# Layer 0 of a graph network: states sent to DRAM node by node, a ring filled from there, and one tile of states for two early blocks

## The chip, the cores and the metric

The kernel runs on one core of one Trainium2 chip. The metric is the device time of one execution in microseconds; 3351.88 us is the median of three runs of the kernel before (3350.82 to 3364.95). The profile is of one more execution of the same kernel.

## The reference

Four layers over 64 graphs of 256 nodes with 256 features; each layer is followed by a residual sum and a layer norm. Layers 1 to 3 are a graph convolution and two attention layers over whole graphs. The change lies in layer 0, a recurrence over the nodes:

```python
def step(h, i):
    x = jnp.take(h_e, i, axis=1)
    row = jnp.take(norm_adjT, i, axis=1)
    x_par = jnp.einsum('bj,bjd->bd', row, h)
    iou = x @ W_ioux.T + b_ioux + x_par @ W_iouh.T + b_iouh
    r, z = jnp.split(iou, 2, axis=1)
    r, z = (jax.nn.sigmoid(r), jax.nn.sigmoid(z))
    hc = jnp.tanh(x @ W_coux.T + b_coux + x_par * r @ W_couh.T + b_couh)
    h_new = z * x_par + (1.0 - z) * hc
    h = jax.lax.dynamic_update_slice(h, h_new[:, None, :], (0, i, 0))
    return (h, None)
```

Node i needs the sum over all nodes j of adj[j, i] times the state of j, where nodes after i still hold their input x. So the steps can't be taken side by side: each needs the new states of all nodes before it.

## The kernel before, in words

`_recurrence` runs 256 steps, one a node, for all 64 graphs at once. A step's tile is 128 partitions by 128 columns: the 64 graphs twice, once for each half o of the 256 features. A step is a chain over TensorE, ScalarE and VectorE: transpose xp, product for the gate r, sigmoid, transpose, product for the candidate, tanh, and the next xp.

Nodes go in blocks of U = 8 (p is the place of a node in its block) and in tables of T = 32. The sum over earlier states that a node needs is put together from four sources:

- **x side** (`x_side`): nodes that still hold their input. For nodes 128 to 255 it is worked off in gaps between the steps of the first ninety or so nodes.
- **near pushes** (`push`, `push_far`): the last nine or more states, added on VectorE and GpSimd as soon as they exist.
- **late side** (`late`, line 491): for each block, a window of up to 64 states before it, by TensorE matmuls that read the ring Hw. It is done in the places p = 0 to 3 of the block before. Its result goes to DRAM (Lb, line 501) and back in another layout (line 507), and is added at p = 6 and 7 (line 876).
- **early side** (`early_*`, lines 365 to 450): all older states, for a whole table k of 32 nodes at a time. States of a range lo to hi are loaded from DRAM (Hd) into Hs for 8 graphs at once (a "piece" t of 8), the adjacency into A for 16 graphs, multiplied in the places p = 4 to 7, stored to Es and read back later by block. A piece's step number in the list says from when on it may be loaded. Tables 4 and 6 both use states 0 to 80, tables 5 and 7 both 0 to 112; each table loads its own Hs.

The ring Hw holds the last 64 states: 64 rows for graphs 0 to 31 and 64 rows for graphs 32 to 63, one state a partition in each half. A new state hs has the graphs on the partitions, so writing it to the ring turns 64 partitions of 512 bytes into two rows; it takes two DMAs, one for each half of the features (`into_ring`, line 652). Since the late side reads the ring at p = 0 to 3, states are queued in `ring_in` and written two a step at p = 4 to 7. Every 32 steps `flush` (line 634) copies 32 states from the ring to Hd, from where the early side and layers 1 to 3 read them. The last eight states go from hs to Hd.

All these DMAs, but for some at the start, are issued by one queue, SP, in the order of the program. Loads that can wait stand in a list (`load_later`) and are taken two a step at p = 0 to 3 (`next_load`, line 870); stores stand in `transfers` and are issued at the end of a step. The order within a step is written out by hand; nothing moves it. Pools give the buffers: hs has 7, Hs and the layers' weights share 4 of tag "wide".

`_layers` then takes the graphs one by one, several in flight in a fixed rotation; each loads its states from Hd into y (line 1045).

Of the kernel before, what the change touches and what calls it, by code (L numbers as in the profile page):

```python
# [9 lines left out]
F32 = mybir.dt.float32  # L10
# [60 lines left out]
def _recurrence(tc, ident, Hd, x, adj, W_ioux, b_ioux, W_iouh, b_iouh, W_coux, b_coux, W_couh, b_couh, wide, then):  # L71
# [32 lines left out]
    with ExitStack() as ctx:  # L104
# [9 lines left out]
        window = [const.tile([P, T], F32, name=f"window{w}") for w in range(2)]  # L114
        dinv = const.tile([P, N], F32, name="dinv")

        Hw = const.tile([P, HB, D], F32, name="Hw")

        def ring(lo, hi):

# [201 lines left out]
        def x_side():  # L322
# [39 lines left out]

        early = [
            (n, k, lo, hi, t)
            for n, k, lo, hi in (
                (25, 2, 0, 16), (57, 3, 0, 48), (89, 4, 0, 80), (121, 5, 0, 112), (89, 6, 0, 80),
                (153, 6, 80, 144), (121, 7, 0, 112), (185, 7, 112, 176),
            )  # L370
            for t in range(B // GB)
        ]
        early_in = []
        early_pb = []
        early_ub = []
        Es = {}

        def early_load(e, got=[]):

            _, k, lo, hi, t = early.pop(e)  # L380
            rows = hi - lo
            if t == 0:
                Es[k, lo] = dram.tile([2, NG, 4, T, P], F32, name=f"Es_{k}_{lo}", bufs=1)
            Hs = wide.tile([P, GB, D], F32, tag="wide", name=f"Hs_{k}_{lo}_{t}")
            last = [load_later(
                Hs[0:rows], Hd[lo:hi, t * GB:(t + 1) * GB, :], 1
            )]
            if t % 2 == 0:
                A = stream.tile([P, 2 * GB, T], F32, tag="A", name=f"A_{k}_{lo}_{t}")
                last.append(load_later(  # L390
                    A[0:rows],
                    adj[t * GB:(t + 2) * GB, lo:hi, k * T:(k + 1) * T].rearrange("b j i -> j b i"), 1
                ))
                got[:] = [A]
            early_in.append((last, k, lo, hi, t, Hs, *got))

        def early_ahead(n):
            ready = [e for e, piece in enumerate(early) if piece[0] <= n]
            if len(early_in) < 4 and ready:

                half = [e for e in ready if early[e][4] % 2 and early[e - 1:e] != [
                    early[e][0:4] + (early[e][4] - 1,)
                ]]
                early_load((half + ready)[0])

        def early_fill(n):

            if early_pb:
                pb, e = early_pb.pop(), 1
            else:  # L410
                if not early_in or not landed(early_in[0][0], n):
                    return False
                _, k, lo, _, t = early_in[0][0:5]
                pb, e = base_bank([P, 2, D], f"early_{k}_{lo}_{t}"), 0
                early_pb.append(pb)
            _, k, lo, hi, t, Hs, A = early_in[0]
            for q in range(4):
                nc.tensor.matmul(
                    pb[q * T:(q + 1) * T, e, :], A[0:hi - lo, t % 2 * GB + e * 4 + q, :],
                    Hs[0:hi - lo, e * 4 + q, :], start=True, stop=True,  # L420
                )
# [69 lines left out]
        def late(first):  # L491

            k, i = divmod(first, T)
            An = tables[k]["An"]
            lb = stream.tile([P, NG, D], F32, tag="lb", name=f"lb_{first}", bufs=1)
            Lb = dram.tile([2, NG, 4, U, P], F32, tag="Lb", name=f"Lb_{first}")
            sides[first] = blk.tile([P, U, P], F32, tag="late", name=f"late_sb_{first}", bufs=1)

            def send():
                for c in range(2):  # L500
                    nc.sync.dma_start(
                        Lb[c].rearrange("n q u f -> (q u) n f"),
                        lb[i // U::T // U, :, c * P:(c + 1) * P],
                    )

            def receive():
                nc.sync.dma_start(sides[first], Lb.rearrange("c n q u f -> (c n q) u f"))

            def then(n):
                at_step(n, send)  # L510
                at_step(n + 1, receive)

            n = yield
            for u in range(0, NG // 2, 2):
                pb = [base_bank([P, 2, D], f"late_{first}_{u}_{g}") for g in range(2)]
                for e in range(2):
                    for q in range(4):
                        for g in range(2):
                            rows = slice(g * W, (g + 1) * W)
                            b = (u + e) * 4 + q  # L520
                            nc.tensor.matmul(  # L521
                                pb[g][q * T:(q + 1) * T, e, :],
                                An[rows, b].rearrange("p u s -> p (u s)"),
                                Hw[rows, b, :], start=True, stop=True,
                            )
# [105 lines left out]
                    acc[:, 0, :], keep[:, j % 2, :], s, acc[:, 0, :], ALU.mult, ALU.add  # L631
                )

        def flush(lo, hi):

            for lo, hi, at in ring(max(lo, 0), hi):
                for g in range(2):
                    nc.sync.dma_start(
                        Hd[lo:hi, g * HB:(g + 1) * HB, :],
                        Hw[g * W + at:g * W + at + hi - lo],  # L640
                    )

        def state(n):

            h = keep[:, n % 2, :]
            nc.vector.tensor_add(h, zcc, keep[:, 2, :])
            hs = new("hs", n, 7)
            nc.vector.tensor_add(hs, zcc, keep[:, 2, :])
            ring_in.append((n, hs))
            return hs  # L650

        def into_ring():
            n, hs = ring_in.pop(0)
            for o in range(2):
                to = Hw[n % W::W] if n < N - U else Hd[n]
                nc.sync.dma_start(to[..., o * P:(o + 1) * P], hs[o * B:(o + 1) * B])

        def push_far(j, hs, first, count):

# [11 lines left out]
        sides = {}  # L671
        xqT = {}
        pushes = []
        ring_in = []

        tables[0]["S"], double = load_S(0)
        double()
# [79 lines left out]
        for now in range(N):  # L757
# [9 lines left out]
            if n:  # L767

                assert all(j == n - 2 for _, j in pushes)
                hs = state(n - 1)  # L770
                end = min((n - 1) // U * U + 2 * U, N)
                to = list(range(n + 1, end))
                near = to[:len(to) - min(FAR[p], len(to) - 1)] if to else []
                far = to[len(near):]
                pushes += [(m, n - 1) for m in near]
                pushes.sort()
                if p == 0:

                    behind = [(n - 1, hs, m, 4) for m in range(end, min(end + U, N), 4)]

                if p > 3 or n >= N - U:
                    for _ in range(min(2, len(ring_in))):
                        into_ring()
            if p == 0 and U < n + U < N:
                late_side = late(n + U)
                next(late_side)
# [97 lines left out]
                sums_in(n // U + 3)  # L884
            if p == 2 and n // U + 2 < N // U:
                xq[n // U + 2] = load_x(n // U + 2)
            if i == 24:
                flush(n - 8 - T, n - 8)
            if n == N - U + 3:
                assert all(j >= N - U for j, _ in ring_in)  # L890
                flush(N - T // 2, N - U)
            if n == N - 5 * U:
                assert not early and not early_in and not loads
                then(lambda to, of: load_later(to, of, 3))
# [10 lines left out]
                if i == 28:  # L905
                    tables[k + 1]["Sd"] = chain_S(k + 1)
        state(N - 1)
        while ring_in:
            into_ring()


def _layers(tc, ident, Hd, Yd, x, adj, weights, out):
# [16 lines left out]
    with ExitStack() as ctx:  # L929
# [92 lines left out]
        class Graph:  # L1022
# [7 lines left out]
            def load(self):  # L1030
# [11 lines left out]
                            adj[b, :, at:at + 32].rearrange("(i r) c -> r i c", r=32),  # L1042
                        )
                self.y = io.tile([P, 2, D], F32, tag="y", name=f"y_{b}", bufs=7)
                nc.sync.dma_start(self.y, Hd[:, b, :].rearrange("(c p) d -> p c d", p=P))


            def residual_0(self):
# [374 lines left out]
def kernel(ctx: ExitStack, tc: tile.TileContext, ins, out):  # L1423
# [4 lines left out]
    dram = ctx.enter_context(tc.tile_pool(name="dram", bufs=1, space=bass.MemoryType.DRAM))  # L1428
    ident = main.tile([P, P], F32, name="ident")
    make_identity(nc, ident)  # L1430
    Hd = dram.tile([N, B, D], F32, name="Hd")
    l2, l3 = (
        {w + n: ins[f"{l}_gnn_{w}{n}"] for w in "Wb" for n in "vkqo"} for l in ("L2", "L3")
    )
# [55 lines left out]
```

## Time and profile before

| | |
|---|---|
| median of 3 runs | 3351.88 us |
| profiled execution, its own time | 3353.51 us |
| its span | 3351.7 us |
| TensorE busy | 3131.6 us, 93% |
| VectorE busy | 2554.5 us, 76% |
| ScalarE busy | 1838.6 us, 55% |
| GpSimd busy | 1845.0 us, 55% |
| DMA moved | 364.62 MB, 528608 packets |
| queue q1 (SP), share of 16 engines | 39.6% |
| HBM read, written | 240.78 MB, 99.61 MB |

The span is the time from the first to the last instruction of the core. The profile's slices are a fortieth of it, 83.8 us each. In the row of TensorE's busy tenths the first sixteen or seventeen slices are layer 0 and its setup (7 to 9 tenths), the rest layers 1 to 3 (9 tenths). The DMA row is 4 to 8 tenths in layer 0 and 1 to 2 in the layers after it. Busy time says little where a chain of small instructions waits for one another, as in layer 0; there, the lengths of single steps and the waits in them are the thing to read.

### The profile page before, as it was taken

What the parts mean: (1) busy time and instruction counts of PE and PEld (TensorE: products, weight loads), DVE (VectorE), ACT (ScalarE), POOL (GpSimd) and SP (SyncE); (2) the same over time, 40 slices, a digit from 0 to 9 for tenths busy, and PEclk for the clock granted to TensorE, in tenths of its full rate; (3) what the DMA queues carried; (4) which work ended last, traced back from release to release, by engine and by line L of the source; (5) the groups of instructions that cost most, each with busy time, mean ns of one, the idle gap of its engine ahead of it and who ended that gap; (6) DMA issues with size and microseconds to landing.
All of it is one profiled execution on the core that took longest, in us unless ns stands there. A gap on an engine that the chain in (4) does not pass through costs nothing.

```text
span 3351.7 us, 78940 instructions
## 1 busy us (share of the span) xinstructions
PE 3131.6 (93%) x28584; PEld 2311.5 (69%) x28584; DVE 2554.5 (76%) x7381; ACT 1838.6 (55%) x4754; POOL 1845.0 (55%) x2165
## 2 busy tenths in 40 slices
PE   5799998998879998969999999999999999999997
PEld 4566665555545555547888888888888888888885
DVE  3487777776667878856888888888888888888885
ACT  0155554544445544535666666666666666666664
POOL 2377777766667878833444444444444444444443
PEclk7899999999999999989999999999999999999999
DMA  9856685788877675241221211122222222222210
GB/s 292 247 161 156 168 194 152 179 198 207 204 181 178 163 174 152 65 105 47 56 57 54 57 56 54 54 55 58 57 58 58 58 57 58 57 58 58 58 33 20
DMA packets 528608, 364.62 MB, mean 109 GB/s; under 512 B 246620, under 2 KB 494568, under 8 KB 522984
## 3 DMA queue, kind: packets, MB, share of 16 engines
q1 hardware_dynamic: 510520, 342.63, 39.6%
q10 hardware_dynamic: 17696, 16.91, 1.5%
q8 instruction: 229, 3.75, 0.5%
q14 instruction: 163, 1.34, 0.1%
HBM read 240.78 MB, written 99.61 MB: 102 GB/s over the span
## 4 chain that ended last, share of the span: by engine, by line
PE 77%; DMA 8%; DVE 7%; issue 2%; SPq 2%; ACT 2%; POOL 1%; DVEq 0%; ACTq 0%; POOLq 0%
PE mm L997 14%; PE rc L605 6%; PE rc L597 4%; PE s L1195 4%; PE mm_2f L997 3%; PE mm_3v L997 3%; PE mm_3f L997 3%; PE mm_2v L997 3%; PE late L521 3%; PE mm_t L997 3%; PE mm_2s L997 3%; PE mm_g L997 3%; PE mm_2w L997 3%; PE o L1230 3%; DVE ACC L630 3%; PE o L1221 3%
## 5 line engine op out<-in xcount | busy, mean ns | idle before, releaser
L1207 POOL TENSOR_TENSOR p3s<-p 128x256 f32<-128x256 f32 x512 | 358.9, 733 | 364.7 <-ACT p L1205 364.6
L630 DVE SCALAR_TENSOR_TENSOR ACC<-keep,S,ACC 128x128 f32<-128x128 f32 x1712 | 479.1, 343 | 16.9 <-POOL ACC L876 11.2
L997 PE MATMUL mm<-xT,weights 128*128 128x256 f32 x2048 | 483.7, 384 | 2.7 <-ACT xT L1094 2.7
L997 PEld LDWEIGHTS mm<-xT,weights 128*128 128x128 f32 x2048 | 386.0, 191 | 79.9 <-issue 25.5
L1204 DVE TENSOR_TENSOR p<-s,neg 128x512 f32<-128x512 f32 x512 | 317.6, 682 | 118.2 <-PE s L1195 118.2
L667 POOL TENSOR_TENSOR ACC<-ACC,far 128x384 f32<-128x384 f32 (+1 forms) x313 | 372.1, 1189 | 24.5
L663 POOL TENSOR_TENSOR far<-hs,S 128x384 f32<-128x384 f32 (+1 forms) x313 | 304.7, 973 | 4.7
L1205 ACT ACTIVATE p<-p 128x512 f32<-128x512 f32 x512 | 292.4, 626 | 1.6 <-DVE p L1204 1.6
L961 ACT ACTIVATE y<-y,shift,rstd 128x256 f32<-128x256 f32 x512 | 272.9, 599 | 26.6 <-DVE shift L959 22.7
L597 PE MATMUL rc<-WxT,xqT 128*64 128x256 f32 x2048 | 274.8, 390 | 1.1 <-issue 1.1
L1119 ACT ACTIVATE qk<-mm,weights 128x256 f32<-128x256 f32 x256 | 107.5, 471 | 301.9 <-PE mm L997 301.9
L805 POOL TENSOR_TENSOR ready<-ACC,dinv 128x128 f32<-128x128 f32 x255 | 102.1, 400 | 304.7 <-DVE ACC L630 304.2
L1108 POOL TENSOR_TENSOR y<-y,g 128x512 f32<-128x512 f32 x64 | 81.0, 1266 | 301.8 <-issue 301.8
L1244 DVE RECIPROCAL rT<-o 128x256 f32<-128x256 f32 x128 | 223.7, 1748 | 0.3 <-PE o L1221 0.2
L949 DVE BATCH_NORM_STATS2 st<-y 128x6 f32<-128x256 f32 x512 | 209.6, 409 | 13.1 <-POOL y L1108 10.3
L521 PE MATMUL late<-Hw,An 64*32 64x256 f32 x3840 | 166.7, 400 | 42.1 <-DMA Hw<-hs 18.8
L605 PE MATMUL rc<-WhT,rT 128*64 128x128 f32 x2048 | 172.5, 290 | 35.6 <-DVE rT L828 33.2
L824 ACT ACTIVATE rs<-rc 128x128 f32<-128x128 f32 x256 | 71.1, 278 | 245.0 <-PE rc L605 245.0
L605 PEld LDWEIGHTS rc<-WhT,rT 128*64 128x64 f32 x2048 | 109.1, 138 | 133.2 <-DVE rT L828 110.8
L953 POOL TENSOR_TENSOR rstd<-rstd,mhalf 128x2 f32<-128x2 f32 x256 | 173.8, 697 | 47.9 <-DVE rstd L952 34.6
L1066 POOL TENSOR_TENSOR dis<-dis,mhalf 128x2 f32<-128x2 f32 x64 | 44.9, 702 | 273.2 <-DVE dis L1065 261.8
L605 PE MATMUL rc<-WhT,xpT 128*64 128x128 f32 x2048 | 169.4, 286 | 18.1 <-ACT xpT L614 18.1
(162 smaller groups left out, 7255.4 us busy)
## 6 DMA issues: line engine op xcount, KB each, us to landing
xX<-in_x_dram ACTq DMA_DIRECT2D x16, 1024.0 KB
Us<-xu SPq DMA_DIRECT2D x64, 256.0 KB
xq<-in_x_dram SPq DMA_DIRECT2D x64, 256.0 KB
ACC<-Us SPq DMA_DIRECT2D x32, 512.0 KB
Es<-eu SPq DMA_DIRECT2D x64, 256.0 KB
early_sb<-Es SPq DMA_DIRECT2D x32, 512.0 KB
xin<-in_x_dram SPq DMA_DIRECT2D x64, 256.0 KB
ad<-in_adj_dram SPq DMA_DIRECT2D x64, 256.0 KB
```

The source lines that it names most:

```text
L521: nc.tensor.matmul(pb[g][q * T:(q + 1) * T, e, :], An[rows, b].rearrange("p u s -> p (u s)"), Hw[rows, b, :], start=True, stop=True,)
L597: nc.tensor.matmul(G[o * B:(o + 1) * B], xqT[a, i // 2][:, i % 2, kc, h * B:(h + 1) * B], WxT[:, kc, o, gates], start=False, stop=False, s ...
L605: nc.tensor.matmul(G[o * B:(o + 1) * B], hT[:, kc * B:(kc + 1) * B], WhT[:, kc, o, g], start=False, stop=(kc == 1), skip_group_check=True,)
L630: nc.vector.scalar_tensor_tensor(acc[:, 0, :], keep[:, j % 2, :], s, acc[:, 0, :], ALU.mult, ALU.add)
L663: nc.gpsimd.tensor_mul(tmp[:, 0:count, :], hs.unsqueeze(1).to_broadcast(shape), s.unsqueeze(2).to_broadcast(shape),)
L667: nc.gpsimd.tensor_add(acc, acc, tmp[:, 0:count, :])
L961: nc.scalar.activation(y[:, c, :], y[:, c, :], AF.Identity, bias=shift[:, c:c + 1], scale=rstd[:, c:c + 1],)
L997: nc.tensor.matmul(pm[:, c, :], lhsT[:, k, c * P:(c + 1) * P], rhs[:, k, :], start=(k == 0), stop=(k == 1),)
L1204: nc.vector.tensor_add(p, s_ps[i], self.neg3)
L1205: nc.scalar.activation(p, p, AF.Exp, scale=ISQ)
L1207: nc.gpsimd.tensor_add(both, p[:, 0, :], p[:, 1, :])
L1244: nc.vector.reciprocal(rT, o_ps[:, 1, :])
```

## The change

1. A new state is sent to Hd as soon as it exists, in one DMA. Hd's layout is now node, feature half, graph, 128 features, so that this is 128 runs of 512 bytes into one contiguous piece of 64 KB. `flush` is gone, and hs has 5 buffers.
2. Of the eight states of a block only the two made at p = 5 and 6 go from hs to the ring, each a step later. The other six are read back from Hd: four at p = 4, two at p = 6. The ring has the feature half outermost, like Hd.
3. The early side keeps up to four tiles of states; a tile loaded for a pair of tables serves both. Pieces are taken in an order written out by hand, pairs of pieces for the two tables in turn. A range is ready as soon as its last state can be in Hd: from n = 18, 50, 82, 114, 146, 178 on.
4. Matmuls that read Hw and Hs take their 256 columns as two runs of 128. Each graph's y is loaded in two DMAs instead of one.

```diff
-        Hw = const.tile([P, HB, D], F32, name="Hw")
+        Hw = const.tile([P, 2, HB, P], F32, name="Hw")
...
-        early = [
-            (n, k, lo, hi, t)
-            for n, k, lo, hi in (
-                (25, 2, 0, 16), (57, 3, 0, 48), (89, 4, 0, 80), (121, 5, 0, 112), (89, 6, 0, 80),
-                (153, 6, 80, 144), (121, 7, 0, 112), (185, 7, 112, 176),
-            )
-            for t in range(B // GB)
-        ]
+        early = []
+        for n, lo, hi, order in (
+            (18, 0, 16, "2222"), (50, 0, 48, "3333"), (82, 0, 80, "46464466"),
+            (114, 0, 112, "57575577"), (146, 80, 144, "6666"), (178, 112, 176, "7777"),
+        ):
+            for e, k in enumerate(order):
+                u = order[:e].count(k)
+                early += [(n, int(k), lo, hi, 2 * u), (n, int(k), lo, hi, 2 * u + 1)]
...
+            if not any(e[0] == (hi, t) for e in states_in):
+                Hs = wide.tile([P, 2, GB, P], F32, tag="wide", name=f"Hs_{hi}_{t}")
+                states_in.append(((hi, t), Hs, load_later(
+                    Hs[0:rows], Hd[lo:hi, :, t * GB:(t + 1) * GB, :], 1
+                )))
+            _, Hs, begun = next(e for e in states_in if e[0] == (hi, t))
...
         def early_ahead(n):
-            ready = [e for e, piece in enumerate(early) if piece[0] <= n]
-            if len(early_in) < 4 and ready:
...
+            if not early or early[0][0] > n:
+                return
+            _, _, _, hi, t = early[0]
+            units = {(e[1], e[2], e[4] // 2) for e in early_in}
+            if t % 2 == 0 and len(units) > 1:
+                return
+            if len(states_in) >= 4 and not any(e[0] == (hi, t) for e in states_in):
+                old = states_in[-4][0]
+                if any(old == (e[3], e[4]) for e in early_in + early):
+                    return
+            early_load(*early.pop(0))
...
-        def flush(lo, hi):
+        def state(n):
+
+            h = keep[:, n % 2, :]
+            nc.vector.tensor_add(h, zcc, keep[:, 2, :])
+            hs = new("hs", n, 5)
+            nc.vector.tensor_add(hs, zcc, keep[:, 2, :])
+            nc.sync.dma_start(Hd[n].rearrange("o b f -> (o b) f"), hs)
+            return hs
+
+        def into_ring(n, hs):
+
+            for o in range(2):
+                nc.sync.dma_start(Hw[n % W::W, o], hs[o * B:(o + 1) * B])
+
+        def into_ring_from_dram(lo, hi):
 
             for lo, hi, at in ring(max(lo, 0), hi):
                 for g in range(2):
                     nc.sync.dma_start(
-                        Hd[lo:hi, g * HB:(g + 1) * HB, :],
                         Hw[g * W + at:g * W + at + hi - lo],
-                    )
...
+                        Hd[lo:hi, :, g * HB:(g + 1) * HB, :],
+                    )
...
-                if p > 3 or n >= N - U:
-                    for _ in range(min(2, len(ring_in))):
-                        into_ring()
+                if p > 5 and n < N - 2 * U:
+                    into_ring(n - 1, hs)
...
-            if i == 24:
-                flush(n - 8 - T, n - 8)
-            if n == N - U + 3:
-                assert all(j >= N - U for j, _ in ring_in)
-                flush(N - T // 2, N - U)
+            if p in (4, 6) and n < N - 2 * U:
+                into_ring_from_dram(n - (5 if p == 4 else 3), n - 1)
...
-                nc.sync.dma_start(self.y, Hd[:, b, :].rearrange("(c p) d -> p c d", p=P))
+                for c in range(2):
+                    nc.sync.dma_start(
+                        self.y[:, c, :].rearrange("p (o f) -> p o f", o=2),
+                        Hd[c * P:(c + 1) * P, :, b, :],
+                    )
...
-    Hd = dram.tile([N, B, D], F32, name="Hd")
+    Hd = dram.tile([N, 2, B, P], F32, name="Hd")
```

More of the change, by code (lines that the diff above doesn't have):

```diff
@@ L375, in _recurrence, with early_load @@
         early_ub = []
+        early_A = []
+        states_in = []
         Es = {}
-        def early_load(e, got=[]):
-            _, k, lo, hi, t = early.pop(e)
+        def early_load(n, k, lo, hi, t):
             rows = hi - lo
-            if t == 0:
+            if (k, lo) not in Es:
                 Es[k, lo] = dram.tile([2, NG, 4, T, P], F32, name=f"Es_{k}_{lo}", bufs=1)
[L384 to L387, printed above, removed]
+            if not any(e[0] == (hi, t) for e in states_in):
[4 more added lines that the diff above has]
+            _, Hs, begun = next(e for e in states_in if e[0] == (hi, t))
             if t % 2 == 0:
                 A = stream.tile([P, 2 * GB, T], F32, tag="A", name=f"A_{k}_{lo}_{t}")
-                last.append(load_later(
+                early_A[:] = A, load_later(
                     A[0:rows],
                     adj[t * GB:(t + 2) * GB, lo:hi, k * T:(k + 1) * T].rearrange("b j i -> j b i"), 1
-                ))
-                got[:] = [A]
-            early_in.append((last, k, lo, hi, t, Hs, *got))
+                )
+            early_in.append(((begun, early_A[1]), k, lo, hi, t, Hs, early_A[0]))
         def early_ahead(n):
-            ready = [e for e, piece in enumerate(early) if piece[0] <= n]
-            if len(early_in) < 4 and ready:
[L401 to L404, printed above, removed]
+            if not early or early[0][0] > n:
[9 more added lines that the diff above has]
+            early_load(*early.pop(0))
         def early_fill(n):
@@ L419, in early_fill @@
                     pb[q * T:(q + 1) * T, e, :], A[0:hi - lo, t % 2 * GB + e * 4 + q, :],
-                    Hs[0:hi - lo, e * 4 + q, :], start=True, stop=True,
+                    Hs[0:hi - lo, :, e * 4 + q, :], start=True, stop=True,
                 )
@@ L523, in late @@
                                 An[rows, b].rearrange("p u s -> p (u s)"),
-                                Hw[rows, b, :], start=True, stop=True,
+                                Hw[rows, :, b, :], start=True, stop=True,
                             )
@@ L638, in flush @@
                     nc.sync.dma_start(
-                        Hd[lo:hi, g * HB:(g + 1) * HB, :],
                         Hw[g * W + at:g * W + at + hi - lo],
+                        Hd[lo:hi, :, g * HB:(g + 1) * HB, :],
                     )
[L643 to L656, printed above, removed]
         def push_far(j, hs, first, count):
@@ L673, in _recurrence @@
         pushes = []
-        ring_in = []
         tables[0]["S"], double = load_S(0)
@@ L907, in _recurrence @@
         state(N - 1)
-        while ring_in:
-            into_ring()
 def _layers(tc, ident, Hd, Yd, x, adj, weights, out):
```

## The prediction

> **What bounds the kernel now.** I read the slices first, then step lengths, then waits, then the DMA queue. A block is the eight nodes n to n+7, p is the node's place in it. Layer 0 runs from 138.5 us to about 1470 us; the start of each transpose of xp (tile xpT_ps) gives the length of every step. Without stalls they are 5.44, 4.81, 4.81, 4.93, 4.76, 5.22, 4.64 and 4.63 us for p = 0 to 7, so 39.3 us a block. Four blocks (columns: length, busy time of each engine with instructions, granted clock, mean DMA share, GB/s), those of n = 112, 120, 136, 176:
>
> ```profile
> core 0: us, PE busy (x) PEld busy (x) DVE busy (x) ACT busy (x) POOL busy (x), PEclk, DMA share, GB/s
> 717.60:757.10 39.50, 38.84 (x539) 23.98 (x536) 33.47 (x121) 21.48 (x70) 29.87 (x34) 1.00 0.83 201
> 757.10:803.80 46.70, 40.26 (x538) 24.88 (x536) 32.70 (x118) 21.40 (x70) 31.40 (x35) 0.97 0.82 211
> 849.70:903.30 53.60, 43.14 (x541) 25.95 (x537) 31.93 (x114) 21.51 (x70) 31.09 (x34) 0.87 0.81 201
> 1083.40:1122.30 38.90, 34.49 (x474) 22.69 (x472) 33.28 (x121) 19.41 (x66) 32.71 (x36) 1.00 0.44 123
> ```
>
> A good block is TensorE from end to end (38.84 of 39.50 us). A bad one has the same instructions and up to 14 us more. The waits and the issues say what is missing there:
>
> ```profile
> PE late L521 <- DMA Hw<-hs: 18.8, 7, 5.6
> ...
> POOL ACC L876 <- DMA late_sb<-Lb: 13.7, 4, 6.2
> ...
> POOL An L479 <- DMA Hw<-hs: 7.7, 1, 7.7
> ...
> PE late L521 <- DMA Hs<-Hd: 5.5, 2, 4.7
> ...
> PE late L521 <- DMA Es<-eu: 5.2, 1, 5.2
> ```
>
> (waiting instruction, releaser: us in total, times, longest) and, of the DMA issues (number, KB each):
>
> ```profile
> Hw<-hs SPq DMA_DIRECT2D x496, 32.0 KB
> ...
> Hs<-Hd SPq DMA_DIRECT2D x16, 896.0 KB
> Hs<-Hd SPq DMA_DIRECT2D x16, 640.0 KB
> ...
> Hd<-Hw SPq DMA_DIRECT2D x8, 1024.0 KB
> ```
>
> The first late matmuls of p = 0 need the state of p = 6 in the ring, written one step earlier; whatever name the wait has, they start when it has landed. Steps more than 1 us over their length, DMA at fault: p = 0 of n = 64, 72, 96, 104, 120, 128, 136, 152, 160, 200 (2.0, 7.4, 1.0, 6.0, 1.3, 5.2, 7.2, 5.3, 8.0, 4.5: 47.9 us) and later steps of blocks 88 to 192 (late sums, adjacency cuts and early states that come late: 30 us). Near 80 us in all; that is what a transfer change can win.
>
> **Why transfers are late at a mean share of 0.8.** The trace's semaphore record shows four ring writes (64 packets of 512 B each) at n = 14 landing at 4.70, 5.50, 6.23 and 6.98 us into the step: 0.75 us apart. A packet takes 28 ns, so 64 x 28 / 750 = 2.4 are in flight, not 16. The Trainium skill, "DMA: Bandwidth & Descriptors", section "Why a DMA increments its semaphore by 16 and not by 1", gives the reason: a DMA is spread over the largest number up to 16 that divides the slowest dimension of both sides, and from this queue over the lowest-numbered engines. The ring write's far side has two partitions: engines 0 and 1, always. The trace's 2.4 agrees. The same page, "Queues, rings and completion order": an engine takes descriptors in ring order. So a ring write waits on engine 0 behind that engine's share of every earlier load, and completions, not the mean share, decide.
>
> So I add up engine 0's work per block, from packet records of layer 0 (512 B 28 ns, 128 B 16, 4 KB 239, 8 KB 560, 16 KB 1146, 32 KB 2323), a sixteenth of each spread transfer plus the whole of the narrow ones. Block 136: four Hs of 896 KB, 4 x 112 x 560 / 16 = 15.7; 3 MB in 4 KB packets (rows, sums, x, sides) 11.5; 1.5 MB in 512 B (Es, Lb) 5.4; 0.88 MB in 128 B (adjacency) 7.1; ring writes 16 x 0.75 = 12.0. Sum 51.7 us against 53.6 measured. Blocks 96 to 167 together: 422 by this sum, 417 measured. Blocks over 39.3, and by how much, add up to 81 us, as the stall list does. Engine 0 bounds the loaded blocks.
>
> **The change, part by part.**
>
> Ring. Removed: 16 ring writes a block (12.0 us on engine 0). Added: 8 state writes to DRAM, 128 packets over 16 engines, 8 x 128 x 28 / 16 = 1.8 us; 4 direct ring writes, 3.0 us; at p = 4 two reads of four rows, four engines, each row two 16 KB packets, 2 x 2.3 = 4.6 us; at p = 6 two reads of two rows, on engines 0 and 1, again 4.6. Narrow work is 12.2 instead of 12.0: no gain, which the fewer descriptors hide at first sight. At n = 68, 132 and 196 the ring wraps, p = 4 has four reads of one and three rows, 6.9 instead of 4.6.
>
> Flush. Removed: every 32 nodes 2 MB from ring to DRAM, 64 x 2.32 / 16 = 9.3 us in blocks 24, 56, 88, 120, 152, 184, 216.
>
> States. One tile for two early blocks: 32 of 64 loads for k = 4 to 7 from state 0 become 16: 8 x 640 and 8 x 896 KB fewer, 12.6 MB. Their packets become 4 KB, 2 x 239 for 560, some 15% less per byte, if 4 KB packets keep their mean. Loads start at n = 18, 50, ... instead of 25, 57, ...; the x side moves back by up to two blocks, to n = 87, and its last sums are read at n = 105 or later. TensorE, VectorE and ScalarE issue the same number of instructions; fills that lay at n = 76 to 79 now lie at 84 to 87, no sum changes.
>
> Engine 0, before and after, blocks over 39.3 in either: 56: 46.0, 37.0; 64: 38.3, 41.6; 72: 41.0, 38.9; 88: 39.8, 32.9; 96: 43.1, 40.7; 104: 45.2, 43.5; 112: 42.2, 33.0; 120: 51.2, 37.7; 128: 49.3, 46.7; 136: 51.7, 49.3; 144: 47.7, 34.0; 152: 49.9, 37.1; 160: 42.1, 42.8; 184: 40.3, 36.1; 192: 41.2, 44.2; 200: 39.8, 34.5. Overhang 81 us before, 34 after: 47 us less. What is won is the unloaded blocks; the ones with four Hs loads (104, 128, 136, 160, 192) stay over.
>
> New waits. SP issues in order (0.55 to 0.7 us each, one more at p = 0 to 3, where it waits for lb at p = 3 anyway: 168.9 us in total there). At p = 4 the late sums' load follows its store sooner, so SP stands some 2 us for the landing (Lb takes at least 2.5); behind it are ring reads due 15 us later. The p = 6 read waits for a state written a step earlier: landed. But its 4.6 us on engine 0 now lies ahead of the last ring write: read issued 2.7 us into p = 6, data from 3.9 (1.2 us, from a lone write's 2.4 landing), done 8.7, state 6 behind it 10.2, landed 10.7, which is 6.1 us into p = 7. Needed: 4.63 plus the 2.1 us until p = 0's first late matmul, 6.7. Margin 0.6 us (before: landed at 5.7). Where two Es stores precede the read at p = 6, 1.7 us more: about 1 us of stall in the four such blocks not counted above, 4 us. DVE's hs has five buffers for seven, but is sent in its own step, so a reuse is five steps off.
>
> Rest. y loads are 128 instead of 64, 0.5 us of SP a graph of 29 us; SP stands 860 us there waiting for ACT: nothing. Moving operands in two runs of 128 (Hw, Hs): the trace of before has no such matmul; 16 of them take 0.59 us on the path, so the 4,864 take 180; bounded between nothing and 5% of it, 9 us; I take nothing, since nothing in the trace prices a run's length. End of layer 0: one flush of 0.5 MB and eight DMAs fewer, all before the last state; 0 to 1 us.
>
> Sum: -47 + 4 = -43 us on 3353.5 of the profiled execution (span 3351.7), which is 1.6 over the median 3351.88 of the runs: 3309 by the median.
>
> **Rivals.**
>
> A. Almost every stall goes, -72 us, 3280. For it: SP's lag. From n = 69 to 71 it issues 20 DMAs in 15.7 us of a budget of 19; afterwards 15 to 17, and large loads hold its completion slots less often. Against it: 136 keeps four loads of 896 KB.
>
> B. Slower: the p = 6 reads push the last ring write past p = 0's late matmuls in every block. 29 blocks; margin 0.6 us. If a 16 KB packet from DRAM takes 1.9 us beside other loads instead of 1.15, the four on engine 0 cost 3.0 more and stall 2.4 a block, 70 us: 3379. It decides from about 2.2 us later than I reckon, where it eats the 43. Against it: 16 KB at 1.15 us is measured.
>
> C. No change, 3345: the loaded blocks' four Hs in a row set the stalls whatever else goes, and new p = 4 and p = 6 waits take what the flush gave. For it: block 64 stalled 7.4 us with only 38.3 by my sum, so the sum misses bunching within a block.
>
> **Numbers.** Main case 0.55, own range 3290 to 3325; A 0.21; C 0.12; B 0.12. Range 3277 to 3349. Less than 0.5% (17 us) can't be told from no change. Faster 0.78 (main, A, a little of C), same 0.11, slower 0.11.
>
> **What would show it.** Right: blocks 120, 144 and 152 near 39 to 40 us, 128 and 136 still over 43; step p = 0 of 72, 104, 136 shorter; no Hd<-Hw; everything after 1470 us moved, not changed. B: p = 0 over 6 us in unloaded blocks (176, 208, 224), waiting for Hw<-Hd or Hw<-hs. A: block 136 under 41. Wrong: early matmuls or POOL's cuts waiting where they did not, or late matmuls longer than 400 ns.

## The result and the profile after

The changed kernel takes 3415.64 us (median of 4 runs, 3411.04 to 3422.94), the kernel before, run beside it, 3355.27 us (3350.82 to 3364.95). The ratio is 1.0177, with an interval of 1.0156 to 1.0197: slower by 1.8%, where the forecast was 3309 us, faster by 1.3%.

All of it is in layer 0. From the first transpose of xp (node 0) to that of node 248, layer 0 takes 1300.5 us before and 1359.1 us after, 58.6 us more; the spans are 3351.7 and 3409.4 us, so what lies outside is 2051.2 and 2050.3 us. By the node's place p in its block, for n = 8 to 247, what the steps take over the lengths of the prediction is:

| | p = 0 | p = 1 to 3 | p = 4, 5 | p = 6, 7 |
|---|---|---|---|---|
| before | 54.6 | 10.4 | 5.0 | 13.9 |
| after | 108.5 | 3.8 | -9.5 | 40.4 |

Steps 1 to 5 gained 21 us, which agrees with a lighter load on the DMA engines; step 0 lost 54 and steps 6 and 7 lost 27. The windows of five blocks of the changed kernel, those of n = 24, 112, 120, 136 and 176 (columns as in the prediction; the last four answer to the four shown there):

```profile
core 0: us, PE busy (x) PEld busy (x) DVE busy (x) ACT busy (x) POOL busy (x), PEclk, DMA share, GB/s
263.50:319.30 55.80, 44.33 (x530) 27.99 (x528) 30.99 (x113) 22.29 (x72) 29.50 (x32) 0.85 0.44 123
769.10:814.20 45.10, 40.29 (x538) 24.48 (x537) 33.42 (x121) 21.59 (x70) 30.20 (x35) 0.96 0.51 138
814.20:853.20 39.00, 38.70 (x538) 24.02 (x536) 31.39 (x113) 21.41 (x70) 30.85 (x34) 1.00 0.68 181
894.00:943.90 49.90, 40.93 (x538) 24.71 (x536) 31.60 (x113) 21.51 (x70) 30.18 (x34) 0.90 0.84 192
1122.50:1167.40 44.90, 38.05 (x490) 24.03 (x488) 33.16 (x121) 20.10 (x67) 32.70 (x36) 0.92 0.49 132
```

Block 120 went from 46.7 to 39.0 us and block 136 from 53.6 to 49.9, as forecast. But blocks 112 and 176, which were at 39.5 and 38.9 with nothing standing, now take 45.1 and 44.9, at a DMA share of only 0.5. The engines are half idle, and the block still waits for a DMA. The waits of the changed kernel (waiting instruction, releaser: us in total, times, longest):

```profile
PE late L527 <- DMA Hw<-hs: 38.1, 11, 8.2
...
ACT xu L256 <- DMA Us<-xu: 28.7, 5, 11.3
...
ACT eu L256 <- DMA Es<-eu: 22.2, 4, 7.9
...
PE late L527 <- DMA Hd<-hs: 13.8, 2, 9.4
...
ACT eu L256 <- DMA Us<-xu: 3.0, 1, 3.0
```

The late matmuls' wait for the ring doubled (18.8 us before), and ScalarE's copies out of PSUM (line 256) now stand 53.9 us for stores to DRAM. Before, that group was one line:

```profile
ACT xu L256 <- DMA Us<-xu: 3.1, 2, 1.6
```

The third place to look is SyncE's own queue, first before, then after:

```profile
SPq L501 <- ACT lb L256: 168.9, 20, 22.7
...
SPq L656 <- DVE ACC L630: 90.1, 76, 4.3
```

```profile
SPq L646 <- DVE ACC L636: 441.6, 168, 8.3
...
SPq L658 <- DMA Hd<-hs: 67.5, 27, 4.7
SPq L507 <- ACT lb L256: 65.3, 23, 3.8
```

Line 646 is the store of a state. SyncE meets one in every step, and stands there until VectorE has made the state; before, it could issue ahead to step 3 and stood there for lb. Line 658 is a read from DRAM into the ring: 27 times SyncE stood for the state store to land (2.5 us on the mean). The DMA issues show the new traffic (number, KB each):

```profile
Hd<-hs SPq DMA_DIRECT2D x256, 64.0 KB
...
Hw<-Hd SPq DMA_DIRECT2D x52, 128.0 KB
...
Hw<-hs SPq DMA_DIRECT2D x120, 32.0 KB
Hw<-Hd SPq DMA_DIRECT2D x60, 64.0 KB
```

The trace's record of every issue and landing gives, for n = 8 to 239, the mean time from issue to landing: the reads of step 4, 7.5 us (those of 128 KB alone, 8.0); the state store issued behind them at step 5, 8.0 us; the ring writes of step 6, 5.4 us; the 64 KB reads of step 6, 4.5 us. A state store with nothing ahead of it lands in 1.5 us. The last ring write of a block landed 2.50 us into step 0 before and 3.34 us after (means of 29 blocks); it was over 2 us, where the first late matmul would wait, in 15 blocks before and 18 after.

So there were two suspects: **the reads into the ring**, of step 4, of step 6 or both, and **the ub buffers**, which ScalarE's copies wait for (two buffers of tag "ub", in which the sums of the x and early sides stand until their store to DRAM has landed). A third was that **SyncE is tied to VectorE** in every step.

### The profile page after: what moved, and what is told of

Same layout as the page of the kernel before. It is cut to its first block, busy times and chain, and to the rows that moved or that the text cites. A ratio compares the mean times of both kernels' runs of the same rounds, so it can differ in the third digit from the quotient of the medians.

```text
span 3409.4 us, 79048 instructions
## 1 busy us (share of the span) xinstructions
PE 3147.0 (92%) x28584; PEld 2320.1 (68%) x28584; DVE 2551.9 (75%) x7381; ACT 1840.0 (54%) x4754; POOL 1846.0 (54%) x2165
## 4 chain that ended last, share of the span: by engine, by line
PE 77%; DMA 9%; DVE 7%; issue 2%; ACT 2%; SPq 1%; POOL 1%; DVEq 0%; ACTq 0%; POOLq 0%
PE mm L995 13%; PE rc L611 6%; PE rc L603 4%; PE s L1197 4%; PE late L527 4%; PE mm_2f L995 4%; PE mm_3v L995 3%; PE mm_t L995 3%; PE mm_3f L995 3%; PE mm_2v L995 3%; PE mm_g L995 3%; PE mm_2s L995 3%; PE mm_2w L995 3%; PE o L1232 3%; DVE ACC L636 3%; PE tr_x L985 3%
## 5 line engine op out<-in xcount | busy, mean ns | idle before, releaser
L611 PEld LDWEIGHTS rc<-WhT,xpT 128*64 128x64 f32 x2048 | 108.4, 138 | 143.6 <-ACT xpT L620 136.9
L831 DVE TENSOR_TENSOR rT<-rT_ps,xpT 128x128 f32<-128x128 f32 x256 | 74.2, 290 | 169.6 <-PE rT_ps L829 167.1
```

Source lines behind the costliest of these rows:

```text
L611: nc.tensor.matmul(G[o * B:(o + 1) * B], hT[:, kc * B:(kc + 1) * B], WhT[:, kc, o, g], start=False, stop=(kc == 1), skip_group_check=True,)
```

## The experiments

Each ratio is to the kernel before, which ran beside each group of experiments, with medians between 3357.5 and 3359.4 us.

### Which part of the change it is

**direct_ring.** The changed kernel, but no read into the ring: two states a step go there from hs, as before, at steps 4 to 7; the states' stores, the shared tiles and the early side are those of the changed kernel.

```
-            hs = new("hs", n, 5)
+            hs = new("hs", n, 7)
             nc.sync.dma_start(Hd[n]..., hs)
+            ring_in.append((n, hs))
...
-                if p > 5 and n < N - 2 * U:
-                    into_ring(n - 1, hs)
+                if p > 3 and n < N - 2 * U:
+                    for _ in range(min(2, len(ring_in))):
+                        into_ring()
...
-            if p in (4, 6) and n < N - 2 * U:
-                into_ring_from_dram(n - (5 if p == 4 else 3), n - 1)
```

> The changed kernel with one part undone: the ring is filled from hs alone, two DMAs a state, two states a step at p = 4 to 7, and never read back from DRAM. States still go to DRAM node by node, no flush, shared tiles. Theory 1 (the reads from DRAM into the ring hold engines 0 to 3 and everything in ring order behind them): the time falls below the kernel before, 3295 to 3320 us, since engine 0's sum over 39.3 us a block is 26 instead of 81; ScalarE's waits for Us and Es fall from 54 us to under 8. Rival (the store of a state in every step, or the early side's new order, costs the time): it stays above 3385.

Measured: 3373.99 us, ratio 1.0050 (1.0036 to 1.0065). That is in neither theory's band. The reads cost about 42 us more than the writes that took their place, yet without them the kernel is still slower than before, so a second loss is in the rest of the change.

**no_p6_read** and **no_p4_read** take one of the two reads away each; its states are written from hs instead.

```
no_p6_read
-                if p > 5 and n < N - 2 * U:
+                if p > 3 and n < N - 2 * U:
                     into_ring(n - 1, hs)
...
-            if p in (4, 6) and n < N - 2 * U:
-                into_ring_from_dram(n - (5 if p == 4 else 3), n - 1)
+            if p == 4 and n < N - 2 * U:
+                into_ring_from_dram(n - 5, n - 1)

no_p4_read: hs has 7 buffers; states 7, 0, 1, 2 go into ring_in, two of them to the ring at each of steps 4 and 5
-            if p in (4, 6) and n < N - 2 * U:
-                into_ring_from_dram(n - (5 if p == 4 else 3), n - 1)
+            if p == 6 and n < N - 2 * U:
+                into_ring_from_dram(n - 3, n - 1)
```

> The changed kernel without the read at p = 6: the states made at p = 3 and 4 go to the ring from hs; the four-row read at p = 4 stays. Theory 1: SP no longer stands for the state's store (67 us at the ring read's line), p = 0 is shorter, but ScalarE still waits about 50 us for Us and Es stores behind the four-row read: 3360 to 3390 us. If the p = 6 read's wait is the whole loss: under 3330.

> The changed kernel without the read at p = 4: the four states go to the ring from hs at p = 4 and 5; the two-row read at p = 6 stays. Theory 1: stores no longer land 8 to 9 us after their issue at p = 5, the p = 6 read no longer waits for one, ScalarE's waits for Us and Es are under 10 us: 3305 to 3335 us. If the p = 6 read is at fault by itself: over 3370.

Measured: no_p6_read 3388.04 us, 1.0099 (1.0072 to 1.0127); no_p4_read 3357.62 us, 1.0001 (0.9986 to 1.0017). The first lies in its band. Both reads have a part, and the step-4 read, the one that I had thought harmless, has the larger: without it 58 us are gone, against 28 without the other. The two can't be added: both gone gives 42, less than the step-4 read alone. So one may act through the other, and what takes the step-6 read's place costs something too: direct_ring writes two states into the ring at each of steps 6 and 7, no_p4_read one, and the last ring write lands 2.20 us into step 0 there, 1.51 here. no_p4_read also missed its band, by 23 us: something else still stood.

**direct_own_tiles** is direct_ring with the early side of the kernel before: its list of pieces (from n = 25, 57, ...) and a tile of states for each piece, so that only the state stores, the missing flush and the layouts (with the matmuls' two runs and y's two loads) are left of the change.

```
-        for n, lo, hi, order in (
-            (18, 0, 16, "2222"), (50, 0, 48, "3333"), (82, 0, 80, "46464466"),
-...
+        early = [
+            (n, k, lo, hi, t)
+            for n, k, lo, hi in (
+                (25, 2, 0, 16), (57, 3, 0, 48), (89, 4, 0, 80), (121, 5, 0, 112), (89, 6, 0, 80),
+...
```

> As direct_ring, and the early side as in the kernel before (each table loads its own states, old steps): the node-by-node store alone, without flush. Engine 0's sum over 39.3 us a block is 56 against 26 with shared tiles: 25 to 35 us over direct_ring, 3325 to 3350 us. If sharing tiles does nothing: equal to direct_ring within 8 us.

Measured: 3365.20 us, 1.0025 (1.0014 to 1.0035). The expectation had the wrong sign: it is faster than direct_ring by 9 us, although it loads 12.6 MB more. Its waits say why (direct_ring: xu 24.4 us and eu 21.8):

```profile
ACT xu L256 <- DMA Us<-xu: 8.2, 2, 4.7
```

No copy into an eu stands for a store any more. My reading was that not the shared tile but the new list of pieces makes the stores late; pair_wait, below, tests it. The list starts at n = 18, 50, ..., late in the loading steps of a block, so the first half of a pair lands alone, is multiplied at step 6, and its half-filled eu holds one of the two ub buffers until the other half comes in the next block. All x and early sums then go through the one that is left, and every copy waits for the last store. On ScalarE's timeline of the changed kernel at n = 30 (start, length, engine, operation, idle time before it and its releaser):

```profile
299.94 0.26 ACT L864 ACTIVATE rc<-rc 128x128 f32<-128x128 f32 x1 [0.42 <-PE rc L611]
300.11 0.59 ACT L256 COPY xqT<-xqT_ps 128x512 f32<-128x512 f32 x1
305.74 0.59 ACT L256 COPY eu<-early 128x512 f32<-128x512 f32 x1 [5.03 <-DMA Es<-eu]
306.22 0.27 ACT L620 COPY xpT<-xpT_ps 128x128 f32<-128x128 f32 x1
```

Step 30 began at 301.06; behind the standing copy is its xpT, from which the whole step starts.

### The two suspects, each by itself

**pair_wait** lets the early side begin a pair only when both halves have landed. Buffers, loads and sums stay.

```
                 _, k, lo, _, t = early_in[0][0:5]
+                if t % 2 == 0 and not (len(early_in) > 1 and landed(early_in[1][0], n)):
+                    return False
                 pb, e = base_bank([P, 2, D], f"early_{k}_{lo}_{t}"), 0
```

> The changed kernel, except that the early side begins the first piece of a pair only once the states of the second have landed too, so that no half-filled eu holds one of the two ub buffers for a block. Theory that ScalarE's copies, which stand for a store to leave the ub buffers (28.7 + 22.2 + 3.0 us in the rows 'ACT xu', 'ACT eu' of the changed kernel), are on the chain that sets the steps: these waits fall from 54 us to under 12, and the time by 30 to 45, to 3370-3385. Rival, that these steps hide behind the ring at the head of the block anyway: the waits fall, the stall at step 0 of the blocks grows by as much, 3400 or more.

Measured: 3380.71 us, 1.0072 (1.0044 to 1.0100), 35 us less than the changed kernel, inside the theory's band. Its window of block 24 and what is left of the waits:

```profile
261.40:300.30 38.90, 38.61 (x537) 23.88 (x537) 31.13 (x113) 21.41 (x70) 27.70 (x32) 1.00 0.59 164
```

```profile
PE late L529 <- DMA Hw<-hs: 43.2, 11, 8.6
...
ACT xu L256 <- DMA Us<-xu: 21.2, 5, 7.0
```

The block takes 38.9 instead of 55.8 us. In the kernel before it was:

```profile
258.90:298.40 39.50, 38.73 (x515) 24.80 (x515) 31.83 (x113) 21.28 (x70) 31.21 (x34) 1.00 0.67 165
```

ScalarE's waits fell by 33 us, from 53.9 to 21.2 (the band said under 12: the x side's own stores remain), and the excess of steps 6 and 7 from 40.4 to 7.2 us. That of step 0 stayed, 109.8 us: 20 us went at n = 24 and 56, and as much came back at n = 48, 64 and 80, with the x side's sums now at other steps. The ring's wait is untouched, as it should be.

**p4_read_on_pool** keeps the step-4 read as it is and issues it from GpSimd's queue instead of SyncE's.

```
-        def into_ring_from_dram(lo, hi):
+        def into_ring_from_dram(lo, hi, far_q=False):
...
-                    nc.sync.dma_start(
+                    (nc.gpsimd if far_q else nc.sync).dma_start(
                         Hw[g * W + at:g * W + at + hi - lo],
                         Hd[lo:hi, :, g * HB:(g + 1) * HB, :],
                     )
...
+                into_ring_from_dram(n - (5 if p == 4 else 3), n - 1, p == 4)
```

> The changed kernel, except that the step-4 read of four ring rows is issued from GpSimd's queue; step-6 read and all else stay with SyncE. Theory that the read harms by the order of SyncE's queue (stores issued after it land 8 to 9 us late and with them the step-6 read): stores at step 5 land in under 5 us again and the time falls to the 3358 of the kernel without that read, 3355-3380. Rival, that the read harms by the time its 16 KB rows take on four DMA engines, from whichever queue: 3400 or more.

Measured: 3354.81 us, 0.9999 (0.9982 to 1.0015), 61 us less than the changed kernel, the same as with the read gone. Its issues (the last number is the median time to landing, which the view gives for this queue), SyncE's wait and the window of block 176:

```profile
Hw<-Hd POOLq DMA_DIRECT2D x52, 128.0 KB, 6.4
```

```profile
SPq L658 <- DMA Hd<-hs: 11.4, 5, 4.6
```

```profile
1085.90:1125.10 39.20, 35.70 (x490) 23.13 (x488) 33.38 (x121) 19.89 (x67) 33.75 (x38) 1.00 0.56 147
```

The read moves the same rows. Behind it, the state store of step 5 lands in 5.0 us instead of 8.0 (4.2 in no_p4_read, with no such read), the ring writes of step 6 in 2.9 instead of 5.4, SyncE's wait ahead of the step-6 read falls from 67.5 us (27 times) to 11.4 (5 times), and the last ring write lands 1.49 us into step 0 instead of 3.34, over 2 us in 8 blocks instead of 18. Block 176 is back at 39.2 us. So the harm came from the read on SyncE's queue. The Trainium skill, "DMA: Bandwidth & Descriptors", section "Queues, rings and completion order", says that an engine takes the descriptors of a ring in order; the stores that land late behind this read, and sooner when it is issued from another queue, agree with it.

The order in the queue is not all that this edit changes, though. The read is itself faster, 6.4 us against 8.0 (medians of the 128 KB reads). The trace's packets say how: on SyncE's queue 3.2 of the 16 packets of 16 KB were in flight on the mean, and they took 6.6 us from the first to the last; on GpSimd's queue it was 5.1 and 4.4 us (26 blocks without a wrap of the ring). SyncE is also spared two issues a block. The same read on a second queue, but no wider than on SyncE's, was not run, so what the order alone costs, and what the read's crowding on a few DMA engines, stays open.

The chain that fits these numbers is: the step-4 read holds back the store of step 5; the step-6 read needs that state, and SyncE stands for it; the ring writes of step 6 land late behind the step-4 read, those of step 7 are issued late (3.6 us into the step instead of 2.3); the first late matmul of the next block waits.

### Both together, and what is left of the change

**no_p4_pair_wait** and **pool_read_pair_wait** put pair_wait's two lines into no_p4_read and into p4_read_on_pool. **direct_ring_pair_wait** puts them into direct_ring. **pool_read_no_p6** is pool_read_pair_wait with the edit of no_p6_read.

> Both edits that should help: no step-4 read (its four states written from hs, as in no_p4_read, 3357.6) and the early side's pair begun only when both have landed. If the two losses are separate and add, 3357.6 less 30 to 42: 3315-3328, below the kernel before. If the one hides the other: 3340 or more.

> The changed kernel with the two edits of pair_wait and p4_read_on_pool together (the step-4 read issued from GpSimd's queue, the pair of the early side begun when both have landed). The two losses were 35 and 61 us taken one at a time. If they are separate: 3355 less 30 to 38, 3317-3325, below the kernel before. If one hides the other: 3340 or more.

> direct_ring (3374.0: the ring filled from hs alone, a store a step, shared tiles) with the pair of the early side begun only when both have landed. Against direct_own_tiles (3365.2, the early side of before) this is the sharing of the tiles alone, without its wait for the ub buffers. Theory that sharing is worth the 13 MB it saves once that wait is gone: 3374 less 30 to 38, 3336-3344, so 21 to 29 below direct_own_tiles. Rival, sharing is worth nothing at all and only the wait made the difference: 3360-3366.

> pool_read_pair_wait (3325.1) without the step-6 read: the states of steps 4 and 5 are written into the ring from hs as they are made, the step-4 read stays on GpSimd's queue. Theory that the step-6 read lost time only because it waited for a store stuck behind the step-4 read: with that gone, taking it away gives nothing more, 3317-3333. Rival, that the narrow step-6 read itself pushes the ring's last write, worth the 28 us that no_p6_read won: 3292-3305.

| | median us | ratio to before | interval |
|---|---|---|---|
| no_p4_pair_wait | 3322.27 | 0.9893 | 0.9865 to 0.9922 |
| pool_read_pair_wait | 3325.06 | 0.9907 | 0.9872 to 0.9942 |
| direct_ring_pair_wait | 3330.55 | 0.9924 | 0.9897 to 0.9950 |
| pool_read_no_p6 | 3316.66 | 0.9884 | 0.9867 to 0.9902 |

The two losses are separate: taken one at a time they were 35 and 61 us, 96 together, and 91 in pool_read_pair_wait. With both mended, every form beats the kernel before by 27 to 41 us.

How the ring is filled hardly matters then: from hs alone 3331, with the step-6 read 3322, with both reads 3325, with the step-4 read alone 3317, and the intervals overlap. So the step-6 read, which was worth 28 us in no_p6_read, is worth about 8, not told from nothing, once the step-4 read is off SyncE's queue (the theory's band began at 3317, the rival's ended at 3305). This agrees with the theory that it had lost its time by waiting. But the total hides a shift. In pool_read_no_p6 the last ring write lands 0.1 us before step 0 on the mean, in no block over 2 us into it, no late matmul waits for a ring write any more, and the excess of step 0 is 4.9 us instead of 35.0. Step 7 took most of that back, 33.5 instead of 11.5: there GpSimd waits for the late sums to come back from DRAM, first pool_read_pair_wait, then pool_read_no_p6:

```profile
POOL ACC L881 <- DMA late_sb<-Lb: 18.3, 7, 4.9
```

```profile
POOL ACC L881 <- DMA late_sb<-Lb: 36.0, 8, 6.8
```

The early side's part of the change is what pays, once its pairs are whole: direct_ring_pair_wait against direct_own_tiles, 0.9924 against 1.0025, is 35 us (21 to 29 expected). The two differ in the shared tiles, in the order and the first steps of the pieces, and in the wait for a whole pair; no run shares the tiles alone, so what the 12.6 MB themselves are worth isn't shown. A part of the difference is GpSimd's wait for adjacency (An for raw), 30.4 us in direct_own_tiles and 11.9 in direct_ring_pair_wait. Dropping the flush for a store in every step, which with the layouts is what direct_own_tiles has left, gives nothing: 1.0025.

### Is SyncE's tie to VectorE a loss?

**store_on_act** issues the state stores from ScalarE's queue.

```
-            nc.sync.dma_start(Hd[n].rearrange("o b f -> (o b) f"), hs)
+            nc.scalar.dma_start(Hd[n].rearrange("o b f -> (o b) f"), hs)
```

> The changed kernel, except that the store of each state is issued from ScalarE's queue instead of SyncE's, so SyncE no longer waits for DVE's hs in every step and can issue ahead. Theory that this wait costs: 20 to 40 us less, 3375-3395. Rival 1, it costs nothing: within 8 us of 3415. Rival 2, the issue (0.33 us on SyncE) falls on ScalarE, which is on the chain in every step: up to 240 x 0.33 = 80 us more, 3430-3495.

Measured: 3482.69 us, 1.0364 (1.0338 to 1.0390). The number lies in rival 2's band, but not for its reason: steps 1 to 5, in which ScalarE issues as many stores as in the others, grew by 10 us in all, step 0 by 61. The late matmuls stood, and SyncE stood for lb (line 507) and, ahead of the ring writes (line 652), for the stores:

```profile
PE late L527 <- DMA Hw<-hs: 99.8, 19, 11.5
```

```profile
SPq L507 <- ACT lb L256: 194.8, 21, 25.9
SPq L652 <- DMA Hd<-hs: 133.4, 35, 9.2
```

**late_store** is no_p4_pair_wait with the stores of states 0, 1 and 2 kept until step 4.

```
+            if n % U < 3 and n < N - 2 * U:
+                stores.append((n, hs))
+            else:
+                store_state(n, hs)
...
+                while p == 4 and stores:
+                    store_state(*stores.pop(0))
```

> no_p4_pair_wait (3322.3) with the stores of a block's states 0, 1 and 2 kept until step 4, so that SyncE waits for no hs in steps 1 to 3 and can issue ahead there. Theory that the store in every step, which ties SyncE to DVE, costs at the head of the block: 10 to 25 less, 3297-3312. Rival, it costs nothing: 3318-3330, or up to 3340 where the three stores in a row at step 4 delay the ring's writes behind them.

Measured: 3354.77 us, 0.9994 (0.9977 to 1.0011), 32 us more than no_p4_pair_wait, worse than either theory. SyncE's wait for lb in no_p4_pair_wait, and then in late_store:

```profile
SPq L509 <- ACT lb L256: 63.2, 23, 3.8
```

```profile
SPq L509 <- ACT lb L256: 216.9, 24, 15.6
```

SyncE did issue ahead: the load of the sums at step 1 went out 2.6 us earlier in its step, that of x at step 2 3.8 us earlier. They landed later after their issue (8.5 for 7.3 us, 7.7 for 5.8), and the last ring write landed 3.23 us into step 0 instead of 2.34. So neither way of undoing the tie gained anything; both lost. Each also changed something else, the stores' queue and ScalarE's work in store_on_act, the place of three stores ahead of the ring writes of step 4 in late_store. Whether the loss came by that or by the loads' issue ahead, the two runs don't tell apart; that stays open.

## Why the prediction was wrong

A gain near the forecast one was there, in part by other terms than it had, and two costs that it had at nothing were larger. In medians: forecast -43 us; found -33 with both costs mended (pool_read_pair_wait, 3325.1 against 3357.6); the step-4 read in SyncE's queue +61; the half pair in a ub buffer +35.

- **Ring: "no gain", and "The p = 6 read waits for a state written a step earlier: landed."** This is the step that failed. The ring's reads stood in the sum at nothing, and issuing one of them from another queue won 61 us. "Landed" was the only place where the sum asked whether the store would be there, and it was answered without the read queued ahead of that store. The store landed 8.0 us after its issue, not within a step, and SyncE stood 27 times. That wait is a part of it: no_p6_read, which has no such wait, won 28 of the 61. The ring writes of step 6, which stand behind the same read, are another.
- **The step-4 read as 4.6 us of work on engine 0.** Counting it so made it equal to the writes that it replaces. It takes 7.5 us from issue to landing, and what is issued behind it on the queue lands late. A sum of work by block can't see this: it gave 34.0 us for block 144, which took 50.6, and 43.7 with the read on the other queue. Nor had it been borne out by block on the kernel before: 422 for 417 us was an agreement of totals, with 47.7 for 41.1 in block 144 and 41.0 for 47.6 in block 72.
- **"16 KB at 1.15 us is measured."** The packets of 16 KB in layer 0 of the kernel before are those of queue q8, which fetches instructions (128 of them, 1147 ns on the mean). Those of the new reads took 0.82 us at step 6 and 1.28 us at step 4. The price was near by luck.
- **"No sum changes"** for the earlier start of the early side. This is the second step that failed. Instructions were counted, buffers were not: 35 us. Block 24, which the forecast had no reason to look at, took 55.8 us, 39.5 before.
- **The margin of 0.6 us ahead of step 0.** The forecast's last ring write, 6.1 us into step 7, is 1.5 us into step 0. With the step-4 read out of the way it lands there on the mean, 1.49 us; as the change was made, 3.34. That the mean agrees is in part luck, as the blocks lie between 2.5 us ahead of step 0 and 7.0 us into it, and for the kernel before, the 5.7 us of the same working, 1.1 us into step 0, stand against 2.50. (The working also writes 8.7 where 3.9 and 4.6 give 8.5.) A margin of 0.6 us was far too small to be taken as cover.
- **Ring and flush.** With the two costs mended, "no gain" from the ring's own work was right (all forms within 14 us). The flush I had as a gain; direct_own_tiles, where a store in every step takes its place, shows none. The early side's part of the change was worth 35 us by itself, so that the total came near the forecast although the flush gave nothing.
- **What was right.** Blocks 120 and 152 fell to 39.0 and 39.2 us; block 136 stayed long, 49.9 (49.3 forecast). Block 128, forecast to stay over 43, fell to 40.7. The moving operands in two runs cost nothing that shows: the late matmuls took 400 ns before, 413 in the changed kernel, where the granted clock was lower too, and 397 in pool_read_pair_wait. The layers after it took the same time.
- **Rival B** was on the right side, 3379, and its sign appeared: step 0 of blocks 176 and 208 took 11.7 and 11.6 us (224 did not, 5.3). But it blamed the time that the step-6 read's packets take on engine 0, 1.9 us each; they took 0.82. That read alone was worth about 8 us with the other on GpSimd's queue; it was late because SyncE stood for the store of the state that it reads.

## What to carry to other kernels

When a transfer is added to a queue, follow what is issued behind it and ask who waits for those landings; the transfer's own due time says little. When one stall is mended, look where it went: the next wait in line may take most of it back. When an order of work is changed, count which buffers are half full between two steps, since a copy on the chain that waits for a buffer waits for a store's landing. Two losses that act at different places can be mended one by one, and a change that came out slower may hold a gain worth keeping: 3316.66 us with the step-4 read on GpSimd's queue, no step-6 read and whole pairs, 1.2% below the kernel before.

## What the runs showed of the hardware

- Two reads of four rows of 32 KB into the ring, 256 KB in all, took 8.0 us each from issue to landing, and the 64 KB stores issued behind them on the same queue 8.0 us, at a DMA share of about 0.5 in blocks 112 and 176. With the reads on GpSimd's queue, the reads took 6.4 us and the stores 5.0; with no such read the stores took 4.2.
- The same reads ran wider from GpSimd's queue than from SyncE's: 5.1 packets of 16 KB in flight on the mean instead of 3.2, and 4.4 us from the first to the last instead of 6.6.
- Block 24 of the changed kernel, which stalled, had a lower granted clock than the same block without the stall: TensorE was busy 44.33 us for 530 matmuls at 0.85, and 38.61 us for 537 at 1.00 in pair_wait. Of the 16.9 us between the two windows, 5.7 are longer busy time of TensorE. That the stall itself lowers the clock is not shown.
- In late_store, where three state stores were moved to step 4, loads were issued up to 3.8 us sooner and landed up to 1.9 us later after their issue, and the kernel took 32 us more than no_p4_pair_wait.
